# A decoder layer whose attention steps are issued two at a time

## The chip, the core and the metric

The kernel runs on one core of a Trainium2 chip. Five engines work from queues of their own, each strictly in the order in which its instructions were issued: TensorE (PE: matmuls and transposes, results into PSUM), VectorE (DVE), ScalarE (ACT), GpSimd (POOL) and SyncE (SP), which here only issues transfers. They meet through semaphores. PSUM has eight banks of 128 x 512 f32 values. Everything in this kernel is f32. The metric is device time in microseconds; three runs of the kernel before gave 658.26, 658.5 and 661.98, the median 658.5.

## What is computed

The reference is one decoder layer over x, 32 sequences of 128 tokens with 128 features, and a context of the same 32 x 128 tokens with 96 features:

```
x = x + linear_attention(layernorm(x))        # 16 heads of 8; sigmoid(q), sigmoid(k); (q kv)/(q ksum),
                                              # layernorm, gate by (x Wh + bh + beta), Wo, relu
x = x + cross_attention(layernorm(x), ctx)    # 16 heads of 64: softmax(q k / 8) v, then Wo (1024 -> 128) + bo
x = x + ffn(layernorm(x))                     # a shared SwiGLU of width 256, plus for each token
                                              # the best of 8 experts, scaled by sigmoid(its logit)
```

## The kernel before

The 32 sequences are eight groups (`NG`) of four (`GT`). **Cross-attention** is 64 steps, `steps`: for every group two halves of the 16 heads, for every half four sequences; a step is one sequence and eight heads. Each step takes these parts (lines 538 to 655):

- `scores` (570): 8 products q·k, each of 64 rows, two at once on the upper and lower half of the array, into `sc` (two banks); DVE then takes `nmax`, the negated maximum of each head.
- `exponentials` (598): 8 ACT instructions, one a head, from `sc` into `pr`, with their sums.
- `divide` (609): `rs` = 1/sums on DVE, then POOL multiplies all of `pr` by it.
- `turn` (617): 8 transposes of `pr`, `prTa` and `prTb`, copied to `prT` by DVE and ACT.
- `mix` (624): 8 products with the values, 64 output columns each, two at once on the left and right half of the array, into `avp`; DVE copies to `oT`.
- `project` (641): `xyp`, then DVE adds it into x.
- `values` (557), `keys` (538), `queries` (547): one 128 x 512 product each, `vp`, `xkp`, `xqp`, with a copy behind it, for this step or a later one.

Beside the steps run three coroutines: `attention(g)`, the linear attention of a later group (376: `xnTp_a`, `kvp`, `qp`, `stp`, `ndp`, `hp`, `lnTp`, `op`, `eTp`), `prologue(g)`, its second layernorm (521: `xnTp_b`), and `router(g)` of an earlier group (655: layernorm, `x3Tp`, logits `lp`, the one-hot choice, positions by `cp`, and four indirect DMAs from POOL that put tokens into expert order, `xsort`). Each `yield` names the kind of place at which it goes on: "P" for PE work, "E" for evictions from PSUM, "S" for statistics, "M" for multiplications. `place(...)` in the loop of the steps lets every coroutine that waits for that kind do one piece. `InTurn` keeps the order of the Python text on each engine, so the text of the loop (line 1088) is the order on the engines.

In that loop step i does, in this order: place E; `divide(i-1)`; `keys` and `queries` of step i+4; place S; `mix(i-2)`; `scores(i)`; the first four exponentials; `project(i-3)`; place M; `turn(i-1)`; the other four exponentials; `values(i)`; place P.

PSUM: `sc` has two banks of its own (`ps_big`, one buffer), every other product takes one of six single banks in turn (`bank`).

**After the steps** the last group's router runs, then `plan` builds the table of 39 tiles of 128 tokens sorted by expert. Tokens are fetched tile by tile by SP (`xt`), `routed` (917) runs each tile through its expert (`tp`, `rgu`, `ryp`), and POOL scatters the result to `ytok`. The shared FFN (`hidden`, `down`: `gate`, `up`, `yp`) needs nothing of this; it is cut into pieces, and `HEAD = NG - 3` (1140) puts five groups of it ahead of the tiles and three behind, where the scattered rows are gathered (`yg`), added and stored.

Of the kernel before, what the change touches and what calls it, by code (L numbers as in the profile page):

```python
# [15 lines left out]
P = 128  # L16
# [32 lines left out]
def kernel(  # L49
# [52 lines left out]
    ps_big = ctx.enter_context(  # L102
        tc.tile_pool(name="ps_big", bufs=1, space=bass.MemoryType.PSUM)
    )
    dram = ctx.enter_context(
        tc.tile_pool(name="dram", bufs=1, space=bass.MemoryType.DRAM)
    )
    ps_mm = ctx.enter_context(
        tc.tile_pool(name="ps_mm", bufs=6, space=bass.MemoryType.PSUM)
    )  # L110

    def big(name):
        return ps_big.tile([P, 2, 512], F32, tag="big", name=name)

    def bank(name):
        return ps_mm.tile([P, 512], F32, tag="mm", name=name)
# [245 lines left out]
    def transposed(src, n, rows, name):  # L362

        ps = bank(name)
        for t in range(n):
            pe_.transpose(ps[0:rows, t * P : (t + 1) * P], src[:, t, :], ident)
        return ps
# [4 lines left out]


    W = D + HA

    def attention(g):
# [6 lines left out]
        ps = transposed(xn, GT, P, f"xnTp_a{g}")  # L383
# [7 lines left out]
        kvps = []  # L391
        for a in range(2):
            kvp = bank(f"kvp{g}_{a}").rearrange("p (t c) -> p t c", t=2)
            for t in range(2):
                rows = slice((2 * a + t) * S, (2 * a + t + 1) * S)
                pe_.matmul(
                    kvp[:, t, :], lhsT=xnT[:, rows], rhs=wkv_a, start=True, stop=True
                )
            kvps.append(kvp)
# [20 lines left out]
        stps = []  # L420
        for a in range(2):
            stp = bank(f"stp{g}_{a}")[:, 0 : 2 * W].rearrange("p (t c) -> p t c", t=2)
            for t in range(2):
                pe_.matmul(
                    stp[:, t, :],
                    lhsT=ks[:, 2 * a + t, :],
                    rhs=kv[:, 2 * a + t, D : 2 * D + HA],
                    start=True,
                    stop=True,
                )  # L430
            stps.append(stp)
# [11 lines left out]
        nds = []  # L443
        for a in range(2):
            nd2 = bank(f"ndp{g}_{a}")[:, 0 : 2 * W].rearrange("p (b w) -> p b w", b=2)
            for b in range(2):
                t = 2 * a + b
                pe_.matmul(
                    nd2[:, b, :],
                    lhsT=qT[:, t * S : (t + 1) * S],  # L450
                    rhs=st[:, t, :],
                    start=True,
                    stop=True,
                )
            nds.append(nd2)
# [13 lines left out]
        yield "E"  # L469
        an = normalized(att, of, pa, f"n{g}")  # L470
        yield "P"
        hp = bank(f"hp{g}")
        pe_.matmul(hp, lhsT=wh_a, rhs=xnT, start=True, stop=True)
        lnp = transposed(an, GT, P, f"lnTp{g}")
# [6 lines left out]
        op = bank(f"op{g}")  # L481
# [9 lines left out]
        if g not in eT_of:  # L491
            ep = transposed(eg_of[g], GT, DE, f"eTp{g}")
# [19 lines left out]
    eT_of, xnT_of, qk_of = {}, {}, {}  # L512
# [8 lines left out]
    def prologue(g):  # L521

        xr = xg[g]
        yield "S"
        of = statistics(xr, f"b{g}")
        yield "M"
        xn = normalized(xr, of, pe, f"b{g}")

        pool_.tensor_tensor(
            xr, xr, bo_x.unsqueeze(1).to_broadcast([P, GT, D]), ALU.add  # L530
        )
        yield "P"
        xp = transposed(xn, GT, P, f"xnTp_b{g}")
        yield "E"
        xnT_of[g] = pe.tile([P, GW], F32, tag="xnT", name=f"xnT_b{g}")
        act_.copy(xnT_of[g], xp)
# [10 lines left out]
    def queries(g, s, j):  # L547

        cols = slice((4 * s + j) * P, (4 * s + j + 1) * P)
        qp = bank(f"xqp{g}_{s}_{j}")  # L550
        pe_.matmul(qp, lhsT=wq_x[:, cols], rhs=xnT_of[g], start=True, stop=True)
        act_.activation(qk_of[g, s, j][:, 0, :], qp, AF.Copy, scale=QSCALE)
# [17 lines left out]
    def scores(k):  # L570
# [4 lines left out]
        sc = big(f"sc{k}")  # L575
# [22 lines left out]
    def exponentials(k, p):  # L598
        sc, nmax = sc_of[k]
        for j in range(4):  # L600
            act_.activation(
                pr_of[k][:, p, j, :],
                sc[:, p, j * P : (j + 1) * P],
                AF.Exp,
                bias=nmax[:, 4 * p + j : 4 * p + j + 1],
                accum_out=sums_of[k][:, 4 * p + j : 4 * p + j + 1],
            )
# [47 lines left out]
    def router(g, of=None):  # L655

        if g < NG - 1:

            yield "E"
            yield "E"  # L660
            yield "E"
# [22 lines left out]
        dve.tensor_copy(lg.rearrange("p t e -> p (t e)"), lp[:, 0 : GT * NE])  # L684
        top = small.tile([P, GT], F32, tag="top", name=f"top{g}")
# [134 lines left out]
    def down(g):  # L820

        y = bank(f"yp{g}").rearrange("p (t c) -> p t c", t=GT)
        n = GT // 2
        halves = [slice(0, n), slice(n, GT)] if g == NG - 1 else [slice(0, GT)]
        for t in range(GT):
            for c in range(NC):
                pe_.matmul(
                    y[:, t, :],
                    lhsT=act_of[g][:, c, t * S : (t + 1) * S],
                    rhs=wd_f[:, c, :],  # L830
                    start=(c == 0),
                    stop=(c == NC - 1),
                )
        for half in halves:
            yield
            dve.tensor_tensor(xg[g][:, half], y[:, half], xg[g][:, half], ALU.add)

    def shared(groups):


        pieces = []
        for g in groups:
            of = [(g, hidden(g, c)) for c in range(NC)]
            if g != groups[0]:
                of.insert(NC if g == groups[-1] else 1, (g - 1, down(g - 1)))
            pieces += of
        return pieces + [(groups[-1], down(groups[-1]))]
# [18 lines left out]
    def numbers(ap, engine):  # L866

        _, got = nc.values_load_multi_w_load_instructions(
            ap,
            [engine],  # L870
            min_val=0,
            max_val=NROW - P,
            skip_runtime_bounds_check_because="the plan keeps within the regions",
        )
        return got
# [9 lines left out]
    def fetch(i, n):  # L885

        for k, at in enumerate(numbers(table[0:1, i : i + n], mybir.EngineType.SP)):
# [21 lines left out]
    def learn(n):  # L909

        for name, (engine, kind) in ENGINES.items():
            i = len(places[name])
            with tc.issue_after(engine.last.ins):
                some = numbers(experts[0:1, i : min(i + n, NT)], kind)
            places[name].extend(expert_of(w) for w in some)
# [91 lines left out]
    beside = []  # L1007

# [18 lines left out]
    def whole(g):  # L1027
        yield from attention(g)
        yield from prologue(g)
# [56 lines left out]
    beside.append(["S", two, None])  # L1086

    for i in range(len(steps)):
        place("E")
        if i >= 1:  # L1090
            divide(i - 1)
        if 1 <= i < len(steps) - GT:
            if steps[i + GT] not in qk_of:
                keys(*steps[i + GT], dve.tensor_copy)
            queries(*steps[i + GT])
        place("S")
        if i >= 2:
            mix(i - 2)
        scores(i)
        exponentials(i, 0)  # L1100
        if i == 0:
            queries(*steps[GT])
        if i >= 3:
            project(i - 3)
            if i % 8 == 2:
                begin(router(steps[i - 3][0]))
        place("M")
        if i >= 1:
            turn(i - 1)
        exponentials(i, 1)  # L1110
        if i == 0:
            for k in range(3):
                values(k)
        elif i >= 3:
            values(i)
        place("P")
        if i % 8 == 3:
            clear_sorted(i // 8)
            g = i // 8 + 2
            if g < NG:  # L1120
                begin(attention(g), lambda g=g: prologue(g))
        if i == 12:
            load_ffn()
        if i == len(steps) - 4:
# [12 lines left out]

    HEAD = NG - 3  # L1140
    pieces += shared(range(HEAD))
    n = len(steps)
    xr, of = xg[NG - 1], moments(f"c{NG - 1}")

    divide(n - 1)
    place("E")
    moment(xr, of, 0)
    project(n - 3)
    moment(xr, of, 1)
    mix(n - 2)  # L1150
    place("M")
    products()
    finish()
    turn(n - 1)
    place("M")
    products()
    mix(n - 1)
    project(n - 2)
    moment(xr, of, 2)
    project(n - 1)  # L1160
    moment(xr, of, 3)
    assert not beside
# [13 lines left out]
    place("E", "M", "P")  # L1176
# [20 lines left out]
    while pieces:  # L1197
# [3 lines left out]
        if len(pieces) == 2:  # L1201
            learn(EXPERTS)
# [3 lines left out]
    for i in range(NT + 6):  # L1206
        if i == EXPERTS:
            learn(EXPERTS)
        if i < NT:
# [17 lines left out]
    for g in range(4):  # L1227
        added(g, pool_)
        store(g, nc.sync)
    products()  # L1230
    finish()
    products()
    finish()
    added(4, dve)
    store(4, nc.sync)
    while len(pieces) > 2:
        products()
        finish()
    added(5, dve)
    store(5, nc.sync)  # L1240
    added(7, dve)
    products()
    finish()
    finish()
    added(6, dve)
# [4 lines left out]
    store(NG - 1, nc.sync, slice(0, GT // 2))  # L1250
    next(piece, None)
    store(NG - 1, act_, slice(GT // 2, GT))
# [36 lines left out]
```

## Time and profile before

| what | value |
|---|---|
| the profiled execution | 658.17 us, its span on the core 656.1 us |
| granted TensorE clock, mean | 1.000 |
| PE busy | 625.3 us, 4729 matmul passes |
| weight loads (PEld) busy | 455.5 us |
| DVE, ACT, POOL busy | 473.9, 350.3, 250.5 us |
| first `sc` of the first step starts | 34.25 us |
| `sc` of step 8, of step 52, of step 62 starts | 94.79, 456.96, 525.63 us |
| last `xyp` group begins, next product after it | 544.38, 546.29 us |
| first fetch of a tile, first transpose of a tile | 565.07, 574.04 us |
| first shared product behind the tiles | 634.69 us |

Times within the span count from its start. An f32 product appears as two passes, so a 128 x 512 product is "x2". Nearly every instruction is issued through the helper at line 38, so the rows are told apart by tile names (`pr<-sc,nmax` writes `pr`, reads `sc` and `nmax`). The length of a matmul row contains its pipeline's end; the distance between the starts of two rows is what the first took of the engine. The profile's chain of waits gives that distance.

### The profile page before, as it was taken

The page shows a single profiled execution, that of the slowest core. Times are in us where ns is not written, and L with a number is a line of the kernel's source. Part 1 is how long each engine was busy: PE and PEld are TensorE (multiplying, and loading weights), DVE is VectorE, ACT ScalarE, POOL GpSimd, SP SyncE. Part 2 cuts the span into 40 slices and gives each one's busy share as a digit, 9 for nine tenths or more (in the row PEclk, how much of TensorE's full clock was granted, in tenths as well). Part 3 has the DMA queues.
Part 4 walks back from the last instruction along what each step waited for, and adds up shares of the span by engine and source line. Part 5 has one row for each costly group of instructions (what it writes and reads, how often), then busy time and mean ns, then how long its engine had stood idle before and what let it go on. Part 6 is the DMA issues. An engine that isn't in the chain of part 4 may idle for free.

```text
span 656.1 us, 13387 instructions
## 1 busy us (share of the span) xinstructions
PE 625.3 (95%) x4729; PEld 455.5 (69%) x4729; DVE 473.9 (72%) x1297; ACT 350.3 (53%) x1365; POOL 250.5 (38%) x237
## 2 busy tenths in 40 slices
PE   8988999999999999999999999999999999899997
PEld 7546777677667766776677666766667676589974
DVE  5757676878687868787878787877776676556654
ACT  4465666564656465655565556555654552255541
POOL 3224222423442344234423542253244243246653
PEclk9999999999999999999999999999999999999999
DMA  6999700000000000000000000004000002242119
GB/s 157 320 338 349 279 2 1 13 1 1 17 12 2 1 17 12 1 1 18 13 1 2 17 1 1 1 17 129 2 9 9 1 1 81 71 111 69 46 48 253
DMA packets 42787, 39.89 MB, mean 61 GB/s; under 512 B 8657, under 2 KB 32721, under 8 KB 42721
## 3 DMA queue, kind: packets, MB, share of 16 engines
q1 hardware_dynamic: 39040, 33.73, 16.8%
q0 software_dynamic: 2272, 4.72, 2.2%
q10 hardware_dynamic: 1408, 0.59, 0.5%
q8 instruction: 37, 0.61, 0.4%
q14 instruction: 30, 0.24, 0.1%
HBM read 14.37 MB, written 24.66 MB: 59 GB/s over the span
## 4 chain that ended last, share of the span: by engine, by line
PE 63%; DVE 20%; ACT 10%; issue 3%; DMA 2%; POOL 1%; DVEq 0%; SPq 0%; ACTq 0%; POOLq 0%
ACT pr L38 8%; PE sc L38 8%; PE xyp L38 7%; PE avp L38 6%; PE xqp L38 6%; PE vp L38 5%; PE rgu L38 5%; PE xkp L38 5%; DVE nmax L38 4%; PE prTa L38 3%; PE prTb L38 3%; PE ryp L38 3%; PE kvp L38 2%; DVE x L38 1%; DVE oT L38 1%
## 5 line engine op out<-in xcount | busy, mean ns | idle before, releaser
L38 ACT ACTIVATE pr<-sc,nmax 128x128 f32<-128x128 f32 x512 | 182.9, 382 | 170.3 <-DVE nmax L38 170.3
L38 POOL TENSOR_TENSOR pr<-pr,rs 128x1024 f32<-128x1024 f32 x64 | 121.3, 1895 | 252.3 <-DVE rs L38 161.5
L38 ACT ACTIVATION_READ_ACCUMULATOR pr<-sc,nmax 128x1 f32 x512 | 112.8, 220 | 0.0
L38 DVE TENSOR_REDUCE nmax<-sc 128x8 f32<-128x1024 f32 x64 | 78.0, 1219 | 17.3 <-PE sc L38 17.2
L38 PEld LDWEIGHTS avp<-prT,v 128*64 128x64 f32 x1024 | 56.1, 136 | 49.0 <-issue 13.6
L38 PE MATMUL sc<-qk 64*128 64x128 f32 x1024 | 74.5, 285 | 2.8 <-ACT pr L38 2.8
L38 PE MATMUL xqp<-xnT_b,wq_x 128*128 128x512 f32 x128 | 65.9, 599 | 9.8 <-ACT xnT_b L38 9.8
L38 PE MATMUL xyp<-wo_x,oT 128*128 128x128 f32 x512 | 73.9, 288 | 0.0
L38 PE MATMUL avp<-prT,v 128*64 128x128 f32 x1024 | 72.9, 279 | 0.9 <-DVE prT L38 0.5
L38 PEld LDWEIGHTS sc<-qk 64*128 64x128 f32 x1024 | 62.2, 187 | 15.6 <-issue 7.9
L38 PEld LDWEIGHTS xyp<-wo_x,oT 128*128 128x128 f32 x512 | 61.9, 191 | 7.6 <-issue 0.2
L38 PE MATMUL vp<-wv_x,eT 96*128 96x512 f32 x128 | 65.2, 593 | 0.0
L38 PE MATMUL xkp<-eT,wk_x 96*128 96x512 f32 x128 | 65.2, 594 | 0.0
L38 DVE COPY v<-vp 128x512 f32<-128x512 f32 x64 | 43.8, 685 | 18.8 <-PE vp L38 18.8
L38 DVE COPY oT<-avp 128x512 f32<-128x512 f32 x64 | 43.8, 684 | 17.3 <-PE avp L38 16.2
L38 ACT ACTIVATE qk<-xqp 128x512 f32<-128x512 f32 x64 | 39.2, 613 | 28.6 <-PE xqp L38 28.4
L38 PEld LDWEIGHTS xqp<-xnT_b,wq_x 128*128 128x128 f32 x128 | 23.4, 189 | 41.4 <-issue 21.1
L38 POOL DMA_INDIRECT ytok<-yt,rows x39 | 37.3, 955 | 36.0 <-DVE rows L38 34.1
L38 DVE COPY prT<-prTa 128x512 f32<-128x512 f32 x64 | 43.9, 685 | 6.2 <-PE prTa L38 4.2
L38 PE MATMUL prTa<-ident,pr 128*128 128x128 f32 x256 | 39.3, 276 | 4.1 <-POOL pr L38 3.2
L38 PE MATMUL rgu<-xT,wt 128*128 128x128 f32 x312 | 41.5, 276 | 1.2 <-DVE wt L38 1.0
L38 DVE COPY qk<-xkp 128x512 f32<-128x512 f32 x56 | 36.1, 645 | 5.5 <-PE xkp L38 5.5
(155 smaller groups left out, 1023.9 us busy)
## 6 DMA issues: line engine op xcount, KB each, us to landing
xsort<-zeros SPq DMA_DIRECT2D x66, 264.0 KB, 4.1
xt<-xsort SPq DMA_DIRECT2D x39, 66.0 KB, 1.9
yg<-ytok SPq DMA_DIRECT2D x8, 256.0 KB, 4.5
x<-in_x_dram SPq DMA_DIRECT2D x7, 256.0 KB, 7.2
out_dram<-x SPq DMA_DIRECT2D x7, 256.0 KB, 4.5
eg<-in_ctx_dram SPq DMA_DIRECT2D x8, 192.0 KB, 2.9
wdr<-in_L_ffn_rt_down_dram SPq DMA_DIRECT2D x2, 512.0 KB
up<-in_L_ffn_rt_up_dram SPq DMA_DIRECT2D x1, 1024.0 KB
```

The costliest lines, as they stand in the source:

```text
L38: made = getattr(self.engine, name)(*operands, **more)
```

## The change

What it does:

- The loop takes two steps, a and a+1, in one round. In a round PE gets, in this order: `sc` a, `sc` a+1, `avp` a-2, `avp` a-1, `xqp` twice, `xyp` twice, `vp` twice, place P, `turn(a)`, `xkp` twice, place P, `turn(a+1)`. All eight exponentials of a step stand together. `keys` are evicted by ACT, not by DVE. A round holds the places E, S, M, P twice, as two steps did, but at other points between the parts.
- PSUM: two pairs of banks (`pair0`, `pair1`) and four single ones. `sc` of even steps has pair 0, of odd steps pair 1. The linear attention and the second layernorm take the same pairs: pair 0 at the first place P of a round, pair 1 at the second. After the steps the pairs become four more single banks.
- `project` stands ahead of `divide` in a round. The router yields once more, "S", between the logits' copy and the choice.
- `HEAD = NG - 4`: four groups of the shared FFN behind the tiles, four ahead. Three tiles are begun (weights copied, tokens transposed) before the loop of the tiles; the order of stores at the end is new, and the last group ends in three sequences and one instead of two and two.

```diff
-    def big(name):
-        return ps_big.tile([P, 2, 512], F32, tag="big", name=name)
+    def pair(side, name):
+        return ps_pair.tile([P, 2, 512], F32, tag=f"pair{side}", name=name)
...
-            kvp = bank(f"kvp{g}_{a}").rearrange("p (t c) -> p t c", t=2)
+            kvp = kv2[:, a].rearrange("p (t c) -> p t c", t=2)
...
-        sc = big(f"sc{k}")
+        sc = pair(k % 2, f"sc{k}")
...
-    for i in range(len(steps)):
+    for a in range(0, n, 2):
+        both = (a, a + 1)
         place("E")
-        if i >= 1:
-            divide(i - 1)
...
+        for k in both:
+            scores(k)
+        if a:
+            mix(a - 2)
+            mix(a - 1)
+        exponentials(a)
+        for k in both:
+            if k + GT < n and steps[k + GT] not in asked:
+                queries(*steps[k + GT])
         place("S")
+        if a:
+            project(a - 2)
+            project(a - 1)
+            if a % 8 == 0:
+                begin(router(steps[a - 1][0]))
+        divide(a)
         place("M")
+        for k in both:
+            values(k)
+        side["now"] = 0
         place("P")
+        exponentials(a + 1)
...
+        divide(a + 1)
+        place("E")
+        turn(a)
+        for k in both:
+            if k + GT + 2 < n and steps[k + GT + 2] not in qk_of:
+                keys(*steps[k + GT + 2], act_.copy)
+        place("S", "M")
+        side["now"] = 1
+        place("P")
+        turn(a + 1)
...
-    HEAD = NG - 3
+    HEAD = NG - 4
...
+    AHEAD = 3
+    ready = [routed(i, fetched[i]) for i in range(AHEAD)]
```

## The prediction

> **What bounds the kernel now.** I read the page first: busy times, then the granted clock.
>
> ```profile
> PE 625.3 (95%) x4729; PEld 455.5 (69%) x4729; DVE 473.9 (72%) x1297; ACT 350.3 (53%) x1365; POOL 250.5 (38%) x237
> PEclk9999999999999999999999999999999999999999
> ```
>
> TensorE is the engine that sets the end: 95% busy at the full clock, and the page's chain gives it 63%. By this row alone no more than 656.1 - 625.3 = 31 us could be won. The Trainium skill, "Perfetto Trace Analysis", § Identifying the Most-Contended Engine, speaks against that reading: busy time of matmuls says little of the room left, since they overlap. So next the chain of waits between 380 and 410 us, whose second column is what each group took from its start to the next group's:
>
> ```profile
> 396.05 0.86 PE xqp L38 x2
> 396.91 1.02 PE avp L38 x16
> 397.94 1.09 PE sc L38 x16
> 399.03 1.09 PE xyp L38 x8
> 400.12 0.44 PE prTa L38 x4
> 400.55 0.44 PE prTb L38 x4
> 400.99 0.86 PE vp L38 x2
> ```
>
> With `xkp` (0.86) a plain step takes 6.66 us. The single starts inside the groups are 0.109 us apart for `avp`'s pairs, 0.1115 for `sc`'s, 0.112 for `xyp`: eight of them make 0.87, 0.89 and 0.90. What is over, 0.15 + 0.20 + 0.19 = 0.54, is the change of tile form (whole array, column halves, row halves, whole array), three times a step, hidden inside "busy". A step streams in 6.12.
>
> Last the timeline, for the length of eight steps and for the steps of the other engines that the new order puts in front of PE:
>
> ```profile
> 382.14 1.16 PE L38 MATMUL sc<-qk 64*128 64x128 f32 x16
> ...
> 397.39 0.28 DVE L38 BATCH_NORM_STATS2 st_c<-x 128x6 f32<-128x128 f32 x1
> 399.10 0.17 DVE L38 TENSOR_SCALAR var_c<-mv_c 128x4 f32<-128x4 f32 x1
> 399.35 1.01 POOL L38 TENSOR_TENSOR rstd_c<-var_c,nhalf 128x4 f32<-128x4 f32 x1 [0.37 <-DVE var_c L38]
> 401.11 1.10 DVE L38 TENSOR_SCALAR xn_c<-x,mv_c,rstd_c 128x128 f32<-128x128 f32 x4
> 401.69 0.91 PE L38 MATMUL x3Tp<-ident,xn_c 128*128 128x128 f32 x4
> ...
> 421.22 0.16 DVE L38 COPY base<-base 128x8 f32<-128x8 f32 x1
> 422.89 0.35 DVE L38 RECIPROCAL rden<-ndp 128x32 f32<-128x32 f32 x1
> 424.00 0.42 DVE L38 TENSOR_TENSOR att<-ndp,rden 128x256 f32<-128x256 f32 x1
> ...
> 432.48 1.89 POOL L38 TENSOR_TENSOR pr<-pr,rs 128x1024 f32<-128x1024 f32 x1 [2.00 <-DVE rs L38]
> 434.52 1.01 POOL L38 DMA_INDIRECT xsort<-xs,row  x1 [0.16 <-issue]
> 435.84 0.96 POOL L38 DMA_INDIRECT xsort<-xs,row  x1 [0.30 <-issue]
> 448.34 1.16 PE L38 MATMUL sc<-qk 64*128 64x128 f32 x16
> ```
>
> The two `sc` are eight steps apart: 66.2 us. Eight steps at 6.66 are 53.3; the products of the coroutines add 9.7 (`hp` 0.86, `lnTp` 0.44, `op` 0.90, `eTp` 0.44, `xnTp_b` 0.44, `x3Tp` 0.44, `lp` 0.81, `xnTp_a` 0.44, `cp` 0.36, `kvp` 1.73, `qp` 0.86, `stp` and `ndp` 0.98 each). So PE waits 3.2 us in eight steps now.
>
> **The change, part by part.** The sum is made against the profiled execution, 658.17 us, 0.3 under the median of 658.5.
>
> *Two steps in one round.* `sc` stands behind `sc`, `avp` behind `avp`: three changes of form for two steps instead of six. A round of two plain steps is 2 x 6.12 + 0.54 = 12.8 instead of 13.3. No row shows `sc` directly behind `sc`; between nothing saved (13.3) and all of it I take all, since within a group pair follows pair at 0.1115. Worth 2.1 us in eight steps, and with the busy row alone it would be nought.
>
> *New waits.* Four rounds make eight steps: A (a divisible by 8: `hp`, `lnTp`, `op`, `eTp`), B (rest 2: `xnTp_b`, `x3Tp`), C (rest 4: `lp`, `xnTp_a`, `cp`, `kvp`, `qp`), D (rest 6: `stp`, `ndp`). I went through each along the queues. Latencies from the trace: `prTa`'s start to its copy 0.69, that copy 0.60 until DVE goes on, `prTb` to its copy 0.66, DVE or ACT to PE 0.05.
>
> First, pair 1. The linear attention's products at the second P stand just ahead of `turn(a+1)`, their evictions behind it on DVE; and the next odd `sc` needs the pair. PE arrives there 0.88 + 0.1 + 0.99 = 1.97 us after `turn(a+1)` began (eight transposes, change of form, even `sc`). Behind the waiting `sc` stand `avp` and all that follows.
> - D, after `kvp`: DVE does `prT`, the router's nine small operations (421.22 to 422.89: 1.67) and then the two `kv_a` (0.60 + 0.69): 0.69 + 0.60 + 1.67 + 1.29 + 0.05 = 4.3. Wait 2.3.
> - A, after `ndp`: `prT`, then `rden`, `att` twice (422.89 to 424.42: 1.53): 2.87. Wait 0.9.
> - B, after `op` and `eTp`: the built program has `ob` on DVE wait for the copy of `eT` on ACT, which is behind the copy of `prTb`: 0.44 + 0.66 + 0.60 + 0.59 + 0.04 + 0.69 + 0.05 = 3.07. Wait 1.1.
>
> Second, B's `x3Tp`. Statistics and multiplication stand at one place, "S", "M", with only two `xkp` (1.73) as cover. From `turn(a)`: `prT` done on DVE 1.29; statistics 1.71 (397.39 to 399.10); `rstd_c` on POOL 0.25 + 1.01; `xn_c` to the first transpose 0.1 + 0.58; transposes 0.75: 5.7. PE needs 0.88 + 1.73 + 0.44 = 3.05. Wait 2.65; now it is 0.3, because `scores` to `vp` lie between.
>
> Third, POOL. In D two puts stand between `pr` of a and of a+1: 1.90 + 2.42 (from 432.48 + 1.89 to 436.80) + 0.1 + 1.90; `turn(a+1)` waits 0.8. In B the bias add (1.27) stands there too, hidden by the wait for `x3Tp`.
>
> Fourth, `project` ahead of `divide`: the reciprocal of a waits on DVE for both adds of `xyp`, starts 7.9 us into the round, and 0.37 + 1.90 + 0.05 later `pr` is done, at 10.2; PE is there at 9.2 plus its P work. A, C and D have 1 us of that; B has 0.44 and its round is late on DVE: 0.5.
>
> Sum in eight steps: 4 x 12.8 + 9.7 = 60.9 of work, 2.3 + 0.9 + 1.1 + 2.65 + 0.8 + 0.5 = 8.3 of waits: 69.2 against 66.2. As rounds: A 16.35, B 17.95, C 17.0, D 17.9. Steps 8 to 51 are six A, six B, five C, five D: 380.3 us, against 456.96 - 94.79 = 362.2: **+18.1**.
>
> *First eight steps:* the same walk gives 14.3, 14.7, 16.5, 15.7 = 61.2, against 60.5: +0.7. *Steps 52 to 61:* 69.2 against 68.7: +0.5 (the puts cost 1.8 in one round, the forms gain). *From there to the last projection:* 20.0 against 20.7: -0.7.
>
> *Four ACT evictions for DVE's:* `xkp` copies, 0.58 each on ACT (53% busy); in every round ACT is idle before `nmax`: nought. If that cover were gone, 1.2 a round.
>
> *The end.* Fetches start 18.8 us after the last projection (546.3 to 565.07), the first tile is there some 2 later, but PE starts it at 574.04, when the shared pieces ahead are done. With one group (3.44 + 1.78 = 5.2) moved behind, PE is free after about 21: 6.7 earlier for 5.2 later, -1.5. 39 tiles at 1.45 are 56.6, but 574.04 to 634.69 are 60.7; with three begun ahead I take -1.5 (between 0 and -3). The last store halves: -0.5. Together -3.5, bounds 0 and -7.
>
> Total 658.2 + 18.1 + 0.7 + 0.5 - 0.7 - 3.5 = **673 us**.
>
> A rule that speaks against the change: the Trainium skill, "TensorE: Matmul & The Clock Gate", § Why this matters for your kernels, warns of PE gaps over about 3 us, after which the clock halves. Here the longest gap of PE is 1.82 (a wait for `act` at 561.8) and the row shows no drop. The new gaps are 2.65 and 2.3: under it, by row and rule, 673. Should the gate close in each of some eleven, half speed for a window of 3.4 us (the page's figure) costs 1.7 each: an estimate of +19, 692.
>
> **Rivals.** (1) *Odd scores don't wait.* Place: the first product of each odd `sc`. Price: 4.3 us in eight steps. If DVE's evictions were done when PE arrives, eight steps take 64.9, and the total is 673 - 5.5 x 4.3 = 650, faster. It turns at 1.5 us: from 2.8 of the 4.3 hidden on, the kernel is no slower. Against it: DVE is 72% busy, and the copy of `prT` cannot start before the transposes. 0.13. (2) *About half of all new waits is covered*, chiefly `x3Tp`'s: 673 - 5.5 x 2.4 = 660, no change that can be told. 0.15. (3) *The clock drops*, 692 or more: 0.10. That PE's order is not as the text says is excluded: in the built program the two `sc`, the two `avp` stand together.
>
> **How the numbers follow.** Forecast (665 to 685) 0.62, rivals 0.13, 0.15, 0.10. About 1% is what a measurement of this kernel tells from no change. Faster by over 1%: 0.12; within 1%: 0.15; slower: 0.73. Range 652 to 691: below it most of rival 1, above it rival 3; it takes in -7 to 0 at the end and 1.5 us either way in eight steps.
>
> **What would show it.** Eight steps 69 us apart in the start of `sc`; `sc` 2 x 0.99 long in a row with one change of form; PE's waits led by `x3Tp` on `xn_c` (six times 2.6) and odd `sc` on `kv_a`, `ob`, `att`; first `tp` some 21 us behind the last projection. I am wrong if evictions of pair 1 end before PE arrives, if a change of form costs more than 0.54 a step, or if the walk misses a wait that crosses two rounds.

## The result, and the profile after

The changed kernel takes 718.4 us (median; 717.4 to 723.8) against 660.2 for the kernel before (658.3 to 662.5) on the same chip: a ratio of 1.089, 95% interval 1.083 to 1.095. The forecast was 673 with a range of 652 to 691. The direction was right, the size was not: 58 us more instead of 15.

The profiled execution took 723.79 us (span 722.0); it lies 5 us above the median, with a lower clock (0.965; 0.974 to 0.976 in the other executions), so what is read below for the clock is more than an ordinary execution has. The page of the changed kernel: span, busy shares in 40 slices, granted clock, and the chain of waits that ended last, by engine.

```profile
span 722.0 us, 13375 instructions
...
PE   8878999898989899889988998899898978989998
...
PEclk9989999899999999999999999999999988999999
...
PE 65%; DVE 21%; POOL 7%; issue 4%; ACT 2%; POOLq 0%; DVEq 0%; ACTq 0%
```

The same rows of the kernel before:

```profile
PE   8988999999999999999999999999999999899997
...
PE 63%; DVE 20%; ACT 10%; issue 3%; DMA 2%; POOL 1%; DVEq 0%; SPq 0%; ACTq 0%; POOLq 0%
```

Three things are new. PE has eights where it had nines. The clock row has eights, in the third and eighth slice and in the 33rd and 34th; the row rounds, so shorter drops do not show. And POOL carries 7% of the chain instead of 1%.

What PE waited for in the changed kernel (total us, times, longest):

```profile
PE x3Tp L38 <- DVE xn_c L38: 14.7, 7, 2.3
PE prTa L38 <- POOL pr L38: 12.3, 13, 2.1
PE sc L38 <- DVE kv_a L38: 11.3, 6, 2.2
PE xnTp_b L38 <- DVE xn_b L38: 7.3, 8, 1.8
PE sc L38 <- DVE ob L38: 6.5, 7, 0.9
PE cp L38 <- DVE onehot L38: 5.1, 5, 1.0
PE sc L38 <- DVE att L38: 4.8, 6, 0.8
PE hlp L38 <- ACT pr L38: 3.5, 1, 3.5
```

`hlp` is the pair of banks that holds `hp` and `lnTp`. The waits for `xn_c`, `kv_a`, `ob` and `att` are the predicted ones, at nearly the predicted lengths. The waits for `xn_b` and `onehot` and that of `hlp` were not predicted.

The same profile by stage: first `sc` to step 8, to step 52, to step 62, to the end. The columns are length, busy time of PE, PEld, DVE, ACT and POOL, then the mean clock.

```profile
35.39:105.58 70.19, 60.70 (x434) 42.65 (x433) 40.56 (x81) 42.43 (x159) 18.52 (x12) 0.93 0.60 211
105.58:520.07 414.49, 366.22 (x2744) 266.49 (x2743) 295.37 (x721) 236.44 (x884) 140.13 (x108) 0.96 0.04 11
520.07:596.21 76.14, 67.35 (x558) 50.16 (x557) 47.17 (x111) 43.06 (x186) 26.79 (x20) 0.95 0.01 5
596.21:722.00 125.79, 116.94 (x864) 97.57 (x863) 75.19 (x247) 51.67 (x170) 54.23 (x55) 0.99 0.32 89
```

| stage | before | after | measured | predicted |
|---|---|---|---|---|
| to the first `sc` | 34.2 | 35.4 | +1.1 | 0 |
| steps 0 to 7 | 60.5 | 70.2 | +9.7 | +0.7 |
| steps 8 to 51 | 362.2 | 414.5 | +52.3 | +18.1 |
| steps 52 to 61 | 68.7 | 76.1 | +7.5 | +0.5 |
| step 62 to the end | 130.5 | 125.8 | -4.7 | -4.2 |

So the surplus is in the loop of the steps. Two mechanisms fill it: one that the prediction did not have, and one that it gave a chance of 0.10. The end came out as reckoned only in its sum: the last steps took 0.5 us more instead of 0.7 less, and what follows the last projection 5.2 less (109.8 to 104.6) instead of 3.5. That the two errors cancel is luck.

**DVE held by POOL.** DVE, POOL and PE in a round B of the changed kernel (start, length):

```profile
283.52 0.19 DVE L38 RECIPROCAL rs<-sums 128x8 f32<-128x8 f32 x1
283.63 2.74 DVE L38 TENSOR_SCALAR xn_b<-x,mv_b,rstd_b 128x128 f32<-128x128 f32 x4
283.88 1.90 POOL L38 TENSOR_TENSOR pr<-pr,rs 128x1024 f32<-128x1024 f32 x1 [0.43 <-DVE rs L38]
...
285.91 0.84 PE L38 MATMUL xnTp_b<-ident,xn_b 128*128 128x128 f32 x3 [0.81 <-DVE xn_b L38]
```

The same four multiplications before:

```profile
252.31 1.10 DVE L38 TENSOR_SCALAR xn_b<-x,mv_b,rstd_b 128x128 f32<-128x128 f32 x4
```

The four took 1.10 us, now 2.74. One of them is stretched: it ends 0.08 us after `pr`, and the last two follow. The durations of a single one (minimum, median, maximum in ns), before and after:

```profile
L38 DVE TENSOR_SCALAR xn_b<-x,mv_b,rstd_b x32: 331/337/346, 28.4 to 451.8; 128x128 f32<-128x128 f32 x32
```

```profile
L38 DVE TENSOR_SCALAR xn_b<-x,mv_b,rstd_b x32: 296/335/2020, 29.6 to 511.7; 128x128 f32<-128x128 f32 x32
```

The Trainium skill, "SBUF — State Buffer", § SBUF: two separate sides, says that DVE and POOL share one pair of ports, and that it is not divided but locked for a whole instruction, when DVE runs in a two-port mode or reads two operands from SBUF. The rows agree: 0.34 us becomes 1.9 to 2.0 when that multiplication and POOL's of 1.90 us begin within 0.07 us of each other. In the loop of the changed kernel this befell 21 of the 128 normalization multiplications, and six of the eight `eq` of the router's choice (below) were stretched too; every one of the 27 ends 0.05 to 0.08 us after a `pr`. Not everything beside POOL is slow: in the kernel before, 24 of the 64 maxima (`nmax`, which DVE reads from PSUM) overlap a `pr`, and with or without it they take 1.21 to 1.23 us. In the kernel before, no normalization met it; in the changed one `divide(a)` starts POOL directly ahead of place M. The router's choice is caught in the same way in round C, with `cp` behind it:

```profile
307.30 1.90 POOL L38 TENSOR_TENSOR pr<-pr,rs 128x1024 f32<-128x1024 f32 x1 [2.08 <-DVE lg L38]
...
307.91 1.33 DVE L38 TENSOR_TENSOR eq<-lg,top 128x32 f32<-128x32 f32 x1
...
310.08 0.38 PE L38 MATMUL cp<-onehot,before 128*128 128x32 f32 x2 [1.02 <-DVE onehot L38]
```

Before, `eq` took 0.19 us in all eight groups:

```profile
L38 DVE TENSOR_TENSOR eq<-lg,top x8: 191/192/193, 148.4 to 553.4; 128x32 f32<-128x32 f32 x8
```

**The clock.** Round B ends with the wait for `x3Tp`. Stretches of the changed kernel around it (length, busy time by engine, clock):

```profile
285.80:289.20 3.40, 3.29 (x15) 1.89 (x15) 3.33 (x12) 1.76 (x3) 2.62 (x2) 1.00 0.00 0
289.20:292.64 3.44, 1.13 (x7) 0.72 (x7) 1.84 (x9) 0.59 (x1) 1.56 (x2) 1.00 0.00 0
292.64:296.05 3.41, 3.41 (x25) 3.08 (x25) 0.69 (x1) 1.07 (x2) 0.00 (x0) 0.50 0.00 0
296.05:299.50 3.45, 3.45 (x54) 2.92 (x51) 3.22 (x4) 1.90 (x11) 0.00 (x0) 1.00 0.02 5
```

After a stretch in which PE was busy for a third (1.13 of 3.44), the clock is 0.50 for exactly one stretch of 3.41 us. The longest idle time in it is 2.3 us. Such half-speed stretches add up to 51 us in the profiled execution, 29.4 of them in steps 8 to 51; that of the kernel before has none.

### The profile page after: what moved, and what is told of

The parts are those of the page before. It is cut to its first block, busy times and chain, and to the rows that moved or that the text cites. A ratio compares the mean times of both kernels' runs of the same rounds, so it can differ in the third digit from the quotient of the medians.

```text
span 722.0 us, 13375 instructions
## 1 busy us (share of the span) xinstructions
PE 642.8 (89%) x4729; PEld 477.9 (66%) x4729; DVE 480.6 (67%) x1242; ACT 388.0 (54%) x1421; POOL 249.1 (35%) x236
## 4 chain that ended last, share of the span: by engine, by line
PE 65%; DVE 21%; POOL 7%; issue 4%; ACT 2%; POOLq 0%; DVEq 0%; ACTq 0%
PE xqp L38 8%; PE avp L38 8%; PE sc L38 8%; PE xyp L38 8%; PE rgu L38 5%; PE prTa L38 3%; PE vp L38 3%; POOL pr L38 3%; PE xkp L38 3%; DVE v L38 3%; DVE xn_b L38 3%; PE prTb L38 3%; PE ryp L38 2%; DVE xn_a L38 2%; DVE prT L38 2%
## 5 line engine op out<-in xcount | busy, mean ns | idle before, releaser
L38 ACT ACTIVATION_READ_ACCUMULATOR pr<-sc,nmax 128x1 f32 x512 | 120.2, 235 | 0.0
L38 PE MATMUL sc<-qk 64*128 64x128 f32 x1024 | 82.0, 311 | 22.6 <-DVE kv_a L38 11.3
L38 ACT COPY prT<-prTb 128x512 f32<-128x512 f32 x64 | 37.5, 585 | 117.7 <-PE prTb L38 117.1
L38 PEld LDWEIGHTS sc<-qk 64*128 64x128 f32 x1024 | 72.5, 216 | 32.7 <-issue 17.9
L38 PEld LDWEIGHTS xyp<-wo_x,oT 128*128 128x128 f32 x512 | 61.9, 192 | 14.8 <-issue 11.2
L38 PE MATMUL avp<-prT,v 128*64 128x128 f32 x1024 | 64.2, 279 | 0.0
L38 PE MATMUL xyp<-wo_x,oT 128*128 128x128 f32 x512 | 62.7, 276 | 0.5 <-DVE oT L38 0.4
L38 PE MATMUL vp<-wv_x,eT 96*128 96x512 f32 x128 | 60.2, 592 | 0.0
L38 PE MATMUL prTa<-ident,pr 128*128 128x128 f32 x256 | 42.1, 290 | 12.8 <-POOL pr L38 12.3
L38 ACT COPY qk<-xkp 128x512 f32<-128x512 f32 x64 | 37.4, 585 | 25.6 <-PE xkp L38 25.6
L38 PEld LDWEIGHTS prTa<-ident,pr 128*128 128x128 f32 x256 | 31.1, 148 | 24.2 <-POOL pr L38 18.3
L38 DVE TENSOR_TENSOR x<-xyp,x 128x128 f32<-128x128 f32 x64 | 18.5, 291 | 40.5 <-PE xyp L38 40.2
```

The source lines that it names most:

```text
L38: made = getattr(self.engine, name)(*operands, **more)
```

## The experiments

They ran on three other chips, on which the kernel before takes 668 to 671 us (medians). So ratios to the kernel before, measured beside each, are compared with 1.089. The lengths of rounds in the steps come out alike on all of them, while the loop of the tiles waits longer there. The changed kernel itself was not run on these chips; if it is longer there by the same 10 us as the kernel before, its ratio is 1.087, so a difference of a few tenths of a point tells nothing. A to D are the four rounds of the prediction. Without a half-speed stretch they take 16.9, 19.1, 19.1 and 18.1 us in the changed kernel (C as in run 1, since every C of the changed kernel holds part of such a stretch).

**1. Work in place of the wait for `x3Tp`.**

```diff
-        ps = transposed(x3, GT, P, f"x3Tp{g}")
+        ps = bank(f"x3Tp{g}")
+        for _ in range(9 if g < NG - 2 else 0):
+            pe_.matmul(ps[:, 0:P], lhsT=ident, rhs=ident, start=True, stop=True)
+        transposed(x3, GT, P, "", ps)
```

> Nine products on constants (ident by ident, into the bank that x3Tp then overwrites) stand on PE ahead of each of the first six x3Tp groups: 9 x 0.22 = 2.0 us of PE work where PE now idles 2.3 us; nothing else is changed. Theory (the granted clock is halved for one window of 3.41 us after a window in which PE was busy for less than about half of it, and x3Tp's wait makes one such window in every eight steps): the half-clock windows that follow x3Tp (five or six) are gone, each gives back up to 1.7 us, PE's wait for xn_c falls to about 0.3 us a time: about 710 us, mean clock about 0.985. Rival (the clock drops for another reason, for instance a limit on sustained work, or the time is all in waits): the windows stay, clock 0.965 to 0.975, and the time stays at 718 or rises by a few us.

Ratio 1.087 (1.082 to 1.092). The half-speed stretches behind `x3Tp` are gone: B falls from 20.0 to 19.06 us, and C, which held the rest of each stretch, from 19.6 to 20.7 down to 19.08. But a stretch now follows the wait of odd `sc` for `kv_a`, so D rises from 18.1 to 19.7. Half-speed time in steps 8 to 51 falls from 29.4 to 13.7 us, their length from 414.5 to 408.2. So idle time of PE causes the drops, as the theory had it: nothing else was changed. The 8 us that were expected did not come: the ratio is within the interval of the changed kernel's, since drops came up elsewhere, and the profiled execution of the changed kernel was one with more half speed than the others.

**2. The router's second M later.**

```diff
-        place("S", "M")
+        place("S")
         side["now"] = 1
         place("P")
...
         turn(a + 1)
+        place("M")
```

> Only the router's second M is moved: from beside S, ahead of the second P, to behind turn(a+1). xn_c is then made a round's part earlier than x3Tp needs it, which comes at the next round's first P (round C), lp at the round's second P. Theory (x3Tp has no cover because statistics and multiplication stand at one place): wait of x3Tp on xn_c falls from 14.7 us to under 2, the half-clock windows behind it go: 7 x 2.1 + 6 x 1.7 = 25 us less, about 694 us, clock about 0.985. Rival (DVE is the bound in those rounds, so what x3Tp no longer waits for, the next sc, cp or turn waits for): under 8 us less, 711 us or more, with sc, cp or prTa waits grown by as much.

Ratio 1.048 (1.043 to 1.053), about 27 us less. There is no half-speed stretch in steps 8 to 51 (382.3 us), and B falls to 16.4. `x3Tp` had no cover, and its wait cost twice: itself, and the clock behind it. Not all of the gain is its own. The router's choice moved as well: `eq` no longer meets a `pr` (0.19 us in all eight groups), and the wait of odd `sc` for `kv_a` fell from 11.3 to 3.7 us, against a new wait of 5.1 us, `ndp` for `st_a`.

**3. Place E ahead of `turn(a+1)`.** (A place E behind the loop goes with it.)

```diff
         both = (a, a + 1)
-        place("E")
         for k in both:
             scores(k)
...
+        place("E")
         turn(a + 1)
```

> The round's first place E is moved from ahead of the two score groups to between the second place P and turn(a+1), so that kv_a, att, ob and lnT are evicted on DVE and ACT ahead of the two copies of prT, while PE transposes. Theory (odd sc waits because pair 1 is freed behind prT on DVE): PE's waits of sc for kv_a, ob, att (11.3 + 6.5 + 4.8 = 22.6 us) fall to under 3: about 698 us, and a little less if some half-clock windows go with them. Rival (the evictions only change places with prT's copy, and PE then waits for prT at avp or for a bank at turn): the sum of PE's waits falls by less than 10 us, 709 us or more.

Ratio 1.054 (1.049 to 1.059), about 23 us less. No `sc` waits any more for `kv_a`, `ob` or `att`; A falls to 15.8, D to 15.7. The first lines of PE's waits in this kernel:

```profile
PE x3Tp L38 <- DVE xn_c L38: 14.7, 7, 2.3
PE prTa L38 <- POOL pr L38: 12.3, 13, 2.1
PE xnTp_b L38 <- DVE xn_b L38: 8.0, 8, 1.8
```

The price of pair 1 is shown, as predicted.

**4. The second group's pair.** Within the loop it takes the pair of its place.

```diff
-            return pair(side["now"] if fixed is None else fixed, name)
+            free = fixed is None or side["loop"]
+            return pair(side["now"] if free else fixed, name)
...
+    side["loop"] = True
     for a in range(0, n, 2):
```

> Within the loop the second group's linear attention takes the pair that the place gives (pair 0 at the first P) instead of always pair 1, on which the first odd sc still stands. Theory (hlp of group 1 waits 3.5 us for exponentials that ACT is given behind it, and that gap halves the clock from 43.5 to 50.3 us): that wait falls to about 1.6 us, the two half windows go: 1.9 + 3.4 = about 5 us less, 713 us; first to eighth sc 65 us instead of 70.2. Rival (PE only waits elsewhere in the start, the first prTa waits for its exponentials and POOL anyway): under 1.5 us less.

Ratio 1.079 (1.074 to 1.084). The first eight steps take 64.2 us instead of 70.2, without a half-speed stretch: a little more than expected, though here a stretch fell ahead of the first `sc`, which starts 1.5 us later. The changed kernel's PE at this place, and the wait that is gone:

```profile
39.28 1.88 PE L38 MATMUL vp<-wv_x,eT 96*128 96x512 f32 x4
44.65 2.08 PE L38 MATMUL hlp<-xnT_a,wh_a 128*128 128x512 f32 x2 [3.49 <-ACT pr L38]
46.52 1.06 PE L38 MATMUL hlp<-ident,xn_n 128*128 128x128 f32 x4
```

**5. Place M and `divide(a)` change places.**

```diff
-        divide(a)
         place("M")
+        divide(a)
```

> Only place M and divide(a) change places: the four multiplications of a normalization stand ahead of the reciprocal that starts POOL's multiplication of pr, not behind it. In the trace of the changed kernel 27 of the 128 multiplications (xn_a, xn_b, xn_c, xn_n) took 2.0 us instead of 0.33, each while POOL multiplied pr; in the kernel before none did. Theory (the two engines lock each other out of SBUF, and the new order puts one onto the other in rounds A, B and C): none takes over 0.4 us, waits of xnTp_b for xn_b (7.3 us) and of hlp and xnTp_a go, and what stands behind on DVE is up to 1.7 us earlier; rounds A, B, C 0.4, 1.3, 0.5 shorter, about -2.2 us in eight steps, -14 us in all, ratio to before about 1.07. Rival (the long multiplications only lie where DVE had time; pr is now begun 1 us later and turn(a) waits for that instead): under 4 us, ratio 1.083 to 1.095.

Ratio 1.088 (1.084 to 1.091): the rival. (The 27 stretched multiplications of this expectation are the 21 and the six `eq`.) No normalization is stretched and the wait for `xn_b` falls to 0.6 us, but `pr` now starts behind the root on POOL and the four multiplications on DVE:

```profile
PE prTa L38 <- POOL pr L38: 31.6, 26, 2.9
```

12.3 us of that wait became 31.6, while the waits for `xn_c` and `xn_b` fell to 6.7 and 0.6 and that of `cp` went: 39.4 us for the four together before this edit, 38.9 with it. Rounds C and D are 1.1 and 0.9 shorter, A is 0.3 longer, and every B holds a half-speed stretch (33.0 us in steps 8 to 51). So in this order the price was moved, not removed.

**6. `divide(a)` ahead of `project`.**

```diff
         place("S")
+        divide(a)
         if a:
             project(a - 2)
             project(a - 1)
...
-        divide(a)
         place("M")
```

> Only divide(a) is moved ahead of project (behind place S), as it stood in the kernel before. Theory (the reciprocal of a waits on DVE for both adds of xyp although the exponentials have been done for up to 2.6 us): pr(a) is done 0.3 to 2 us earlier, the wait of prTa for pr (12.3 us) falls to 6 or 7 us, chiefly in the rounds at the end that carry no linear attention; ratio about 1.08. Rival (the multiplications of place M still fall under POOL's multiplication of pr, now from its middle, so that the waits for xn_b and xn_c stay): within 0.3% of the changed kernel, 1.086 to 1.093.

Ratio 1.065 (1.060 to 1.070), 16 us less, over twice what was expected. Rounds A, B, C and D are shorter by 0.4, 0.2, 0.4 and 0.9, steps 52 to 61 by 5.0. The multiplications still fall under POOL (21 of them, up to 1.9 us), but later in `pr`, so they are freed sooner. Most of the gain is not the lock's: the 0.9 in each D and the 5.0 in steps 52 to 61 come from rounds with hardly a stretched multiplication, in which `turn` had waited for `pr` itself.

**7. Four edits together, with M ahead of `divide(a)`:** those of 2, 3, 4 and 5.

> Four edits together: the router's second M behind turn(a+1), place E between the second P and turn(a+1), place M ahead of divide(a), and the second group's linear attention on the pair of its place. If they add up as the rounds of each show: A 15.6, B 15.6, C 17.6, D 15.7 us = 64.5 in eight steps against 75.1 in the changed kernel and 66.2 before; first eight steps 62 (60.5 before), steps 52 to 61 73 (68.7 before), end as in the changed kernel, 4.7 shorter than before: a ratio of about 0.99 to 1.00, clock over 0.99. Rival (the rounds have a floor of their own: score, maximum, both sets of exponentials, division and turn of step a+1 lie in one round, 1.0 + 1.2 + 4.9 + 4.9 + 0.4 + 1.9 + 1.0 = 15.3 us and more where anything stands between): no round under 15.7, 67 in eight steps, a ratio of 1.015 to 1.03.

Ratio 1.038 (1.031 to 1.044), beyond the rival's mark: PE waits 45.4 us for `pr`, 32 times, and B swings between 16.2 and 19.1 us with the clock. The floor that the rival named is not what bounds it: the next run has rounds of 15.4.

**8. Four edits together, with `divide(a)` ahead of `project`:** those of 2, 3, 4 and 6.

> As e9_all, but with divide(a) moved ahead of project instead of behind place M: the router's second M late, place E ahead of turn(a+1), the second group's linear attention on the pair of its place, and divide(a) ahead of project. Theory (the four gains lie at different waits and add up: in rounds A to D the single edits took 1.1 + 0.4, 0.7 + 2.7 + 0.2, 0.8 + 0.4, 2.4 + 0.9 us off 16.9, 19.1, 19.1, 18.1): 15.5, 15.5, 17.9, 14.8 = 63.7 us in eight steps without half-clock windows, steps 8 to 51 350 us, steps 52 to 61 71, first eight 62: ratio 0.98 to 0.99. Rival (a floor by the chain within one round, maximum, both sets of exponentials, division and turn of a+1, some 15.3 us and more with the locked multiplications of place M ahead of the second reciprocal): no round under 15.3, 66 in eight steps, ratio 1.00 to 1.02.

Ratio 0.9945 (0.992 to 0.997), between the two marks. Rounds 15.6, 15.4, 18.0, 16.5, where D was to be 14.8; no half-speed stretch in steps 8 to 51, which take 358.5 us (362.2 before). It differs from run 7 only in where `divide(a)` stands, which is worth 4 points. The single gains (4.1, 3.6, 1.0 and 2.4 points) come to more than the 9.5 that they give together: several of them had also taken away some of the same half-speed stretches.

**9. Place S behind the scores, place M and `divide(a)` ahead of `project`.** Run 8, and:

```diff
         for k in both:
             scores(k)
+        place("S")
...
-        place("S")
-        divide(a)
+        place("M")
+        divide(a)
         if a:
             project(a - 2)
...
-        place("M")
```

> As e6_all, but place S stands right behind the two score groups and place M ahead of divide(a), both ahead of project, so that the root on POOL and the four multiplications on DVE are done before POOL multiplies pr. Theory of the lock between DVE and POOL (it is what e6_all still pays): no multiplication over 0.4 us, the waits of xnTp_b, hlp and xnTp_a gone, 2 us less in eight steps than e6_all, ratio some 0.02 below it. Rival (statistics ahead of the copies of avp and the multiplications ahead of the reciprocal delay xyp and pr by as much, as in e8_m_first): prTa waits for pr more, ratio within 0.005 of e6_all or above it.

Ratio 0.988 (0.983 to 0.994); the interval overlaps that of run 8. The lock does not show any more on `xn_b`:

```profile
L38 DVE TENSOR_SCALAR xn_b<-x,mv_b,rstd_b x32: 339/344/348, 29.8 to 444.8; 128x128 f32<-128x128 f32 x32
```

It is not gone altogether. In this kernel, as in runs 2, 7, 8 and 10, another small operation of the router now meets a `pr`, seven times of eight:

```profile
L38 DVE TENSOR_TENSOR pos<-pos,onehot x8: 192/1086/1093, 156.7 to 551.9; 128x32 f32<-128x32 f32 x8
```

The gain in eight steps is only 0.5 us (16.05, 15.1, 18.1, 15.8), not 2: the copies of `avp` now stand behind the statistics on DVE.

```profile
PE xyp L38 <- DVE oT L38: 16.2, 23, 2.6
```

**10. `values` ahead of `project`,** on top of run 9.

```diff
         divide(a)
+        for k in both:
+            values(k)
         if a:
             project(a - 2)
...
-        for k in both:
-            values(k)
```

> As e10_early_s, but values (vp twice, 1.73 us on PE) stand ahead of project instead of behind it. Theory (in e10_early_s the copies of avp stand behind the statistics on DVE, and PE waits for them at xyp: 16.2 us in all, 23 times): vp covers that wait, xyp waits under 4 us, 1.5 us less in eight steps: ratio 0.97 to 0.98. Rival (a round without the wait is bound by its chain, the wait only goes on to turn: prTa waits for pr instead): within 0.4% of e10_early_s.

Ratio 0.978 (0.973 to 0.983): 654.8 us beside 668.0, the best version. The wait of `xyp` falls to 0.7 us. In the steady rounds nothing is won (16.05, 15.1, 18.0, 15.8), as the rival said; PE now waits there for other copies (`vp` for those of `qk`, 7.1 us in all). In the profiled executions the gain lies in steps 52 to 61, 66.3 us instead of 69.5. These two executions are only 2 us apart, the medians 7; the rest is in executions of which no trace was kept. The ratio met the theory's mark, but not by its reason.

## Why the prediction was wrong

**Right.**
- *The odd `sc`.* Longest waits: `kv_a` 2.2 (predicted 2.3), `ob` 0.9 (1.1), `att` 0.8 (0.9); taking the cause away took the waits away (run 3).
- *`x3Tp`.* 2.3 (2.65), and run 2 shows its cause, the missing cover: 0.8 us is left of 14.7 there.
- *POOL's puts in D.* From `ndp` to `turn(a+1)` 0.8 to 1.0 us too much (0.8). Round D was 18.07 against 17.9.
- *Changes of form.* Two steps pay them once: the product groups of a round without waits (from start to start: `sc` 1.99, `avp` 1.90, `xqp` 1.82, `xyp` 1.78, `vp` and `xkp` 1.72 each, the two turns 0.88 and 0.97) add up to 12.78 us (12.8).
- *The end.* First `tp` 21.5 us behind the last projection (21); the sum of -4.7 against -4.2 is in part luck, as said above.

**Wrong**, in steps 8 to 51 (+52.3 instead of +18.1). The rounds without a half-speed stretch, taken six times A and B and five times C and D, make 401.5 us where 380.3 were predicted: 21.2 us are waits, and the other 13.0 up to 414.5 go with the half-speed stretches.

1. *"Fourth, `project` ahead of `divide`"*, 0.5 us in B alone. The step looked at when `pr` is done for PE, and not at what else `pr` holds up. In B the delay at `xnTp_b` is 1.34 us, in A 0.45 at `hlp`, in C 0.52 at `xnTp_a`: each is a multiplication that waits for POOL. Undoing the move brought 16 us (run 6), where the step reckoned some 3; but the larger part of the 16 lies in D and in steps 52 to 61, where `turn` had waited for `pr` itself, so they do not measure the lock.
2. *Round C was given no wait at all.* `cp` waits there 1.0 us by its row, 1.3 by the distance of the starts: `eq` is held 1.33 us by the second `pr`. With the 0.52 of `xnTp_a` that is most of the 2.1 us by which C is longer than 17.0. The walk gave DVE's small operations the lengths that they had before, when `eq` and the normalizations met no `pr`. The share of items 1 and 2 due to the lock is 3.1 of the 3.9 us missing in eight steps, by the distances of PE's rows (0.45 in A, 1.34 less the predicted 0.5 in B, 0.52 and 1.29 in C). This split is read from the trace; no run removed the lock alone without moving something else, and runs 5 and 9 show that much of its price comes back elsewhere if only the order is turned.
3. *The clock was put at nothing, by the length of a gap.* "The new gaps are 2.65 and 2.3: under it" was the wrong test: PE's busy share of the stretch in which the gap lay was a third. Rival 3 came true beside the forecast, not in its stead: at most half of 29.4 us here, 13.0 by the sum, and it goes with the waits (runs 1 and 2). By the other executions' clock it is less in them.

The smaller stages failed in the same manner. *First eight steps:* "the same walk" missed that the second group's linear attention has a fixed pair; `hlp` waits 3.5 us until ACT has read the first odd `sc` out of it, and 6.8 us at half speed follow (run 4: 6.0 us less in this stage). *Steps 52 to 61:* "+0.5" took these rounds for bound by PE. Without linear attention PE reaches `turn` early, and the late `divide` shows in full: `prTa` waits 6.4 us for `pr`, and 7.9 us run at half speed; run 6 takes 5.0 off, run 10 comes to 66.3.

Two steps at a time are thus not slow in themselves: with their parts in another order (run 10) the kernel is 2.2% (1.7 to 2.7) faster than the one before. In its trace the steps up to 61 take 8.4 us less than in the trace before (483.0 and 491.4), some 1.3%; the new end is in every variant too, and no run took it out, nor the move of the `keys` copies to ACT. What made the change slower is where its parts stand.

## What to carry to other kernels

When a loop is reordered, ask of each DVE operation that stays within SBUF which POOL operation it now meets, not only which semaphore it waits for; its old duration holds only in its old neighbourhood. A wait on PE has two prices, its own length and the clock after it; sum PE's busy time over stretches of a few microseconds instead of looking for one long gap. And before a wait is costed, look for everything that stands behind the operation that was moved: the same late `divide` cost 0.2 us in one round (B) and 1.7 in another (a D round without linear attention, 15.7 and 14.0 us).

## What the runs showed of the hardware

- The granted clock follows PE's activity in a fixed grid of 3.41 us: within each trace the starts of the half-speed stretches lie whole multiples of 3.41 apart. Cutting the eleven traces of the changed kernel and its variants into these stretches, from their first half-speed stretch on and back, gives: PE busy under 40%, 27 of 27 followed by half speed; 40 to 50%, 38 of 45; 50 to 60%, 9 of 35; above, 24 of some 2,100, 14 of them second stretches of one drop. The Trainium skill, "TensorE: Matmul & The Clock Gate", § What's actually happening, has the free-running window of 3413 ns, and the runs agree. Its § Why this matters for your kernels, which the prediction used, warns of gaps over about 3 us; here one gap of 2.3 us was enough, since it lay whole within one window (1.13 + 2.31 = 3.44).
- Whether a gap costs clock depends on where it falls in the grid: the wait of 2.2 us for `kv_a` was followed by half speed in two rounds D of five in the changed kernel, and in four of five once the gap before it was filled (run 1).
- A DVE multiplication of 0.34 us took 2.02 beside a POOL multiplication of 1.90, and a DVE comparison of 0.19 took 1.33. The stretched time counts as DVE's busy time in the profile, so no row of DVE's own waits names it: a maximum far above the median in a tile's row is how it is seen.
